# Half of the attention's queries get their scores with keys on partitions

## The chip, the cores and the metric

The kernel runs on one core of a Trainium2 chip. The core has TensorE (PE, the matrix engine, with its weight loads shown apart as PEld), VectorE (DVE), ScalarE (ACT), GpSimd (POOL) and SyncE (SP, which here only issues DMAs); each works through its own instructions in order and waits on semaphores for the others. The metric is the device time of one execution in microseconds (us). Before the change it is 1508.91 us, the median of 3 runs (1508.52 to 1512.15).

## The reference, cut to what matters

The model layer is a linear recurrent unit, a gated feed-forward block, a multi-head attention and the same feed-forward block again, each added to x, which is 4 x 1024 tokens of width 256. The change is in the attention, which has 8 heads of width 64, with keys and values made from one latent of width 64:

```
def _L0_attn_b_ref(x, Wq, Wkv_down, Wk_up, Wv_up, Wo):
    B, T = (4, 512)
    D_MODEL = 256
    N_HEADS = 8
    HEAD_DIM = 64
    ...
    q = (x @ Wq.T).reshape(b, t, N_HEADS, HEAD_DIM)
    kv_latent = x @ Wkv_down.T
    k = (kv_latent @ Wk_up.T).reshape(b, t, N_HEADS, HEAD_DIM)
    v = (kv_latent @ Wv_up.T).reshape(b, t, N_HEADS, HEAD_DIM)
    scale = HEAD_DIM ** (-0.5)
    scores = jnp.einsum('bqhd,bkhd->bhqk', q, k) * scale
    attn = jax.nn.softmax(scores, axis=-1)
    out = jnp.einsum('bhqk,bkhd->bqhd', attn, v)
    out = out.reshape(b, t, N_HEADS * HEAD_DIM)
    return out @ Wo.T
```

Here b is 4 and t is 1024 (the shape of x decides, not the constants). The feed-forward block needs, per token, the 32 largest of 256 softmax scores twice over.

## The kernel before, in words

Everything stays on the chip. There are three stretches: the recurrent unit, the first feed-forward block's first 8 tiles and the attention's weights (to about 356 us); the attention, with the other 24 tiles of the first feed-forward block and the start of the second woven in (to about 1275 us); the second feed-forward block (to the end).

The attention absorbs the key and value matrices into the query and output weights, so that keys and values of all heads are the latent itself. `kh` and `kl` are the rounded latent and its remainder (float32r), with channels on partitions, the 64 channels twice; `qs` holds for each head of a pair the query's rounded part on one half of the partitions and its remainder on the other. So one product with `kh` and one with `kl` sum to almost exact scores.

`heads` (L856) is the main loop. For a batch b, it goes over 2 blocks of 512 queries (nb), 4 pairs of heads (g) and 4 groups of 128 queries (q): 128 units in all, each with two steps, one for each head (j) of the pair; 256 steps in all. A step makes scores `sc` with queries on partitions and 1024 keys in the free dimension (L886, 4 matmuls with 512 columns), their negated maximum `nm` (L890), and the exponentials `pr` with their sum (L894). The value product needs keys on partitions, and here units differ:

- even q (`by_dma`): `pr` is split into two f16 parts `pd` (L897 on ACT, L898 on POOL) and a DMA turns both over (L899, issued by SP) into `d`; the value product takes 48 matmuls in f16;
- odd q: PE turns `pr` over in 8 blocks of 128x128 per step (L905, into `ptp`), ACT copies them out in two halves (L910; in the last batch DVE takes one half, L908), and the value product takes 16 matmuls in f32, which the profile shows as 32.

`values_sum` (L920) does the value product into `pmo` (L930), spreads the reciprocals of the sums over 128 columns (`rows`, L926 on POOL), transposes them on PE (L938), copies them out (L940 on ACT) and multiplies (L941 on DVE) into `on`. It is called some steps after the scores: the lists `pending` and `late` hold back what waits for the copies and for the DMA.

All else in this stretch is side work: `queries` (L842), `output` (L943), `prepare` and `values` for the next batch, feed-forward tiles (`f1.tile`, L589, with its 8 rounds of top-8 in L674, and `nm` on POOL in L613) and `f2.head`. `merge` (L963) sets the order: after each step of `heads` it lets those side generators run whose due step has come, with the due steps written out by hand in L1202 to L1228. The instructions go to the engines through a scheduler that keeps close to this order. PSUM buffers are few: two score buffers `sc` of two banks, two of one bank for turned blocks (`t`), two of one bank for all else (`s`).

## Time and profile before

| what | from | us |
|---|---|---|
| time, median of 3 runs | the times | 1508.91 |
| span of the profiled execution | the page | 1505.6 |
| first stretch, 0 to 356.5 | windows of the trace | 356.5 |
| attention stretch, 356.5 to 1275 | windows of the trace | 918.5 |
| last stretch, 1275 to the end | windows of the trace | 230.6 |

Busy us of each engine in the three stretches, from the same answer:

| stretch | PE | PEld | DVE | ACT | POOL | granted PE clock | DMA share |
|---|---|---|---|---|---|---|---|
| first | 302.23 | 191.71 | 286.50 | 178.25 | 116.94 | 0.95 | 0.17 |
| attention | 822.83 | 655.29 | 689.26 | 704.43 | 429.86 | 0.99 | 0.43 |
| last | 153.37 | 100.30 | 205.19 | 135.31 | 136.17 | 0.82 | 0.06 |

A row of the profile names the line, the engine, the operation, the tile written and those read, the shapes and the count; then the busy time and the mean duration of one; then the idle time of the engine just before such instructions and what ended it. PE's instructions overlap (one starts while the one before it drains), so their mean duration is longer than the distance between them; busy time counts the union.

### The profile page before, as it was taken

Reading aid. Unit: us, or ns where it says so; the run is one execution under the profiler, and the core shown is the slowest. Engines: PE = TensorE matmul, PEld = TensorE weight load, DVE = VectorE, ACT = ScalarE, POOL = GpSimd, SP = SyncE. Lnnn points to the kernel's source line nnn. Section 1 sums busy time; section 2 is a strip of 40 time slices with the busy share of each in tenths; the row PEclk is TensorE's granted clock in tenths of the full one; section 3 lists DMA queues with packets and bytes.
Section 4 is the critical chain, followed back from the end, with each engine's and each line's share of the span. In section 5 each row is a group of like instructions: output and inputs, shape, how many; then the busy total and the mean of one; then the engine's idle time right before and its main releaser. Section 6 shows DMA issues by size and latency. Waiting matters only on the chain. (4 is left out here: it accounts for less than half of the span.)

```text
span 1505.6 us, 28728 instructions
## 1 busy us (share of the span) xinstructions
PE 1278.4 (85%) x10136; PEld 947.3 (63%) x10136; DVE 1181.0 (78%) x3682; ACT 1018.0 (68%) x2152; POOL 683.0 (45%) x849
## 2 busy tenths in 40 slices
PE   4899998887998998898988988889999999576765
PEld 3645555465776777676766766677777877244544
DVE  8988676796778876977777778777676675599998
ACT  5334535666878877787877687877877776566664
POOL 2024523352555454454534543545443534067776
PEclk9999999799999999999999999999999999678898
DMA  3010000432553443353434344433444444000000
GB/s 119 20 55 15 22 21 29 144 105 50 92 88 72 81 86 67 61 89 75 77 73 79 61 69 80 75 74 71 71 85 85 85 85 85 1 15 25 22 25 29
DMA packets 288754, 96.52 MB, mean 64 GB/s; under 512 B 268377, under 2 KB 284770, under 8 KB 288610
## 3 DMA queue, kind: packets, MB, share of 16 engines
q1 hardware_dynamic: 283522, 88.90, 29.6%
q10 hardware_dynamic: 5088, 5.78, 1.1%
q8 instruction: 80, 1.31, 0.4%
q14 instruction: 64, 0.52, 0.1%
HBM read 16.01 MB, written 11.53 MB: 18 GB/s over the span
## 5 line engine op out<-in xcount | busy, mean ns | idle before, releaser
L898 POOL TENSOR_TENSOR pd<-pr,pd 128x1024 f16<-128x1024 f32 x128 | 273.6, 2142 | 259.3 <-ACT pd L897 200.1
L890 DVE TENSOR_REDUCE nm<-sc 128x1 f32<-128x1024 f32 x256 | 308.4, 1217 | 74.8 <-PE sc L886 73.2
L894 ACT ACTIVATE pr<-sc,nm 128x1024 f32<-128x1024 f32 x256 | 286.1, 1120 | 89.8 <-DVE nm L892 54.7
L886 PE MATMUL sc<-kh,qs 128*128 128x512 f32 x512 | 184.4, 438 | 28.5 <-ACT pr L894 21.0
L886 PE MATMUL sc<-kl,qs 128*128 128x512 f32 x512 | 161.7, 396 | 0.0
L674 DVE MATCH_REPLACE8 wk<-m,wk 128x256 f32<-128x256 f32 x384 | 155.3, 408 | 0.1
L910 ACT COPY p<-ptp 128x512 f32<-128x512 f32 x224 | 124.1, 591 | 44.4 <-PE ptp L905 32.5
L674 DVE MAX8 m<-wk 128x8 f32<-128x256 f32 x384 | 150.7, 413 | 0.4
L905 PE MATMUL ptp<-ident,pr 128*128 128x128 f32 x1024 | 139.2, 276 | 13.3 <-ACT pr L894 12.0
L930 PE MATMUL pmo<-p,la 128*64 128x128 f32 x2048 | 140.2, 284 | 5.9 <-ACT ft L524 2.9
L905 PEld LDWEIGHTS ptp<-ident,pr 128*128 128x128 f32 x1024 | 116.2, 141 | 35.5 <-ACT pr L894 21.7
L897 ACT CAST pd<-pr 128x1024 f16<-128x1024 f32 x128 | 133.5, 1054 | 4.6 <-DMA d<-pd 3.6
L930 PEld LDWEIGHTS pmo<-p,la 128*64 128x64 f32 x2048 | 119.6, 142 | 24.7 <-issue 4.7
L886 PEld LDWEIGHTS sc<-kh,qs 128*128 128x128 f32 x512 | 85.2, 195 | 53.9 <-ACT pr L894 32.9
L886 PEld LDWEIGHTS sc<-kl,qs 128*128 128x128 f32 x512 | 96.6, 189 | 23.2 <-issue 1.4
L930 PE MATMUL pmo<-d,lb 128*64 128x128 f16 x3072 | 101.5, 220 | 8.7 <-DVE qs L853 2.6
L930 PEld LDWEIGHTS <-lb 128*64 128x64 f16 x3072 | 90.7, 110 | 26.6 <-issue 19.9
L628 POOL TENSOR_TENSOR ex<-ex,wk 128x512 f32<-128x512 f32 x61 | 77.8, 1276 | 58.4 <-DVE wk L674 48.9
L926 POOL COPY rows<-rs 128x128 f32<-128x128 f32 x128 | 36.3, 297 | 120.4 <-PE pmo L938 71.7
L941 DVE TENSOR_TENSOR on<-pmo,rb 128x128 f32<-128x128 f32 x128 | 36.4, 284 | 64.8 <-ACT rb L940 64.3
L147 PE MATMUL pt<-ident,xn 128*128 128x128 f32 x256 | 48.9, 310 | 44.0 <-ACT xn L145 32.3
L699 PE MATMUL pf<-wf,vt 128*128 128x256 f32 x288 | 80.9, 424 | 3.9 <-ACT vt L697 3.4
(307 smaller groups left out, 2766.1 us busy)
## 6 DMA issues: line engine op xcount, KB each, us to landing
tt<-ft SPq DMA_DIRECT2D x16, 256.0 KB
tt<-tt SPq DMA_DIRECT2D x8, 512.0 KB
out<-x SPq DMA_DIRECT2D x32, 128.0 KB
x<-in_x ACTq DMA_DIRECT2D x6, 512.0 KB
pf<-pfs SPq DMA_DIRECT2D x12, 256.0 KB
full<-pf SPq DMA_DIRECT2D x24, 128.0 KB
d<-pd SPq DMA_TRANSPOSE x128
wa<-in_w_attn SPq DMA_DIRECT2D x2, 640.0 KB
```

Of the source, the lines that this page charges most:

```text
L147: nc.tensor.transpose(pt[:, k, i * P : (i + 1) * P], xn[:, k * P : (k + 1) * P], ident)
L628: pool.tensor_tensor(ex, ex, wk, ALU.subtract)
L674: ins = make(*args).ins
L699: nc.tensor.matmul(dst, vt[:, k, :], w.wf[:, k, :], start=(k == 0 and bias is None), stop=(k == KD - 1))
L886: nc.tensor.matmul(sc[:, sl], qs[:, j, q * P : (q + 1) * P], kk[:, sl], start=(i == 0), stop=(i == 1))
L890: nc.vector.tensor_reduce(nm, sc, AX.X, ALU.max, negate=True)
L894: nc.scalar.activation(pr, sc, AF.Exp, bias=nm, accum_out=ssum[:, j : j + 1])
L897: nc.scalar.copy(pd[:, 0, :], pr)
L898: nc.gpsimd.tensor_tensor(pd[:, 1, :], pr, pd[:, 0, :], ALU.subtract)
L905: nc.tensor.transpose(pt[:, kk, :], pr[:, kc * P : (kc + 1) * P], self.ident)
L910: nc.scalar.copy(dst, pt)
L930: nc.tensor.matmul(po[j * HD : (j + 1) * HD, 0, :], v, pts[j][:, c, :], start=(n == 0), stop=(n == len(terms) - 1),)
```

## The change

Even units stay as they were in what they compute. Odd units (q of 1 and 3) are made differently, in a new class `Turned`:

- `maxima`: a step's scores with queries on partitions, but with `kh` alone (2 matmuls where there were 4), and their negated maximum;
- `begin`: four DMAs on SP's queue build `bq`, 65 partitions of moving data: the rounded queries of both heads on 64 partitions, and on the 65th the negated maxima, which go to DRAM (128 partitions of 2 elements) and come back as one row of 256;
- `chunks`: scores a second time, with keys on partitions and the 2 x 128 queries of both heads in the free dimension: for each block of 128 keys one matmul with `kh` as weights against `qs` and one with `kb` (the 64 channels of `kl` and a row of ones) against `bq`, so that the last contraction row subtracts the maximum. ACT makes the exponentials of two blocks at a time, in f32, directly where the value product needs them; POOL adds the four results into `acc`;
- `values`: the value product from these, 16 matmuls as before, and a copy of the undivided result into `on`.

For both odd units of a group together, `sums` adds `acc` over partitions with a matrix of ones (8 matmuls), takes reciprocals, and spreads them with 8 DMAs into `rb`; `divide` multiplies `on` on POOL. `heads` is replaced by `sweep`, which runs over all 32 groups (a batch, a block and a pair) of 8 steps, with the place of each piece written out: for group n, at step t = 8n, maxima at t, t+2, t+4, t+6, `begin` at t+2.1 and t+6.1, chunks from t+5.1 and t+9.1 on, one per step, values at t+9.5 and t+13.5, sums at t+14.05; the last group has its own places. The due steps of the side work move with it, and `latents` copies `kl` into `kb` by DMA.

The diff, cut; the class `ByDma`, not shown, holds the even units' part of the old loop (with 2 buffers of `pr` for 3), and `values_sum`, now called for even units only, is unchanged.

```diff
+        self.ones = wp.tile([P, 32], F32, tag="ones32", name="ones32")
+        self.nc.gpsimd.memset(self.ones, 1.0)
...
+                wp.tile([HD + 1, T], F32R, tag="kb", name="kb", bufs=2),
             )
+            nc.gpsimd.memset(self.k[b][4][HD : HD + 1, :].bitcast(F32), 1.0)
...
+        nc.sync.dma_start(self.k[b][4][0:HD, to].bitcast(F32), kl[0:HD, to].bitcast(F32))
...
-    def heads(self, b, psum):
...
+    def sweep(self, psum):
+        groups = [(b, nb, g) for b in range(B) for nb in range(2) for g in range(PAIRS)]
+        events = []
+        def at(time, make, *args):
+            events.append((time, len(events), make, args))
+        for n, key in enumerate(groups):
+            t = 8 * n
+            last, before = n == len(groups) - 1, n == len(groups) - 2
+            for i, q in enumerate((0, 2)):
+                unit = self.by_dma(*key, q)
+                for j in range(2):
+                    at(t + (2 * i + j if last else 4 * i + 2 * j + 1), unit.scores, j, psum)
+                at(t + (5 + 2 * i if last else 7 + 4 * i), unit.values, psum)
+            units = [self.turned(*key, q) for q in (1, 3)]
+            for i, unit in enumerate(units):
+                for j in range(2):
+                    at(t - 2.5 + i + 0.5 * j if last else t + 4 * i + 2 * j, unit.maxima, j, psum)
+                at(t + 0.2 + 4 * i if last else t + 2.1 + 4 * i, unit.begin)
+                for c in range(TPB // 2):
+                    at(t + 3 + 2.6 * i + 0.5 * c if last else t + 5.1 + 4 * i + c, unit.chunks, c, psum)
+                at(t + 5 + 2.3 * i if last else t + 9.5 + 4 * i, unit.values, psum)
+            at(t + 8.3 if last else t + 14.05, self.sums, units, psum)
+            at(t + 8.4 if last else t + 14.1 if before else t + 15.95, self.divide, units)
+        events.sort(key=lambda e: e[:2])
+        for step in range(8 * len(groups)):
+            while events[0][0] < step + 1:
+                _, _, make, args = events.pop(0)
+                make(*args)
+            yield
+        for _, _, make, args in events:
+            make(*args)
...
+    def sums(self, units, psum):
+        nc, sp = self.nc, self.sp
+        ps = psum.tile([P, P], "s", "pss")
+        for half in range(2):
+            for i, unit in enumerate(units):
+                for j in range(2):
+                    r = 64 * j + 32 * i
+                    nc.tensor.matmul(
+                        ps[r : r + 32, :], self.ones, unit.acc[:, half, j, :], start=half == 0, stop=half == 1
+                    )
+        rec = sp.tile([P, P], F32, tag="rec", name="rec", bufs=1)
+        nc.vector.reciprocal(rec, ps)
+        rb = self.rb = self.hp.tile([P, 2, P], F32, tag="rb2", name="rb2", bufs=1)
+        for i in range(2):
+            for j in range(2):
+                for half in range(2):
+                    to, of = 64 * j + 32 * half, 64 * j + 32 * i
+                    nc.sync.dma_start(rb[to : to + 32, i, :], rec[of : of + 32, :])
+    def divide(self, units):
+        for i, unit in enumerate(units):
+            self.nc.gpsimd.tensor_tensor(unit.on, unit.on, self.rb[:, i, :], ALU.mult)
...
+class Turned:
...
+    def begin(self):
+        at, nc = self.at, self.at.nc
+        qs = at.qs[self.key]
+        self.bq = at.hp.tile([HD + 1, 2, P], F32R, tag="bq", name="bq", bufs=2)
+        for j in range(2):
+            mine = slice(j * HD, (j + 1) * HD)
+            nc.sync.dma_start(
+                self.bq[0:HD, j, :].bitcast(F32), qs[mine, j, self.q * P : (self.q + 1) * P].bitcast(F32)
+            )
+        rows = at.dram.tile([2, P], F32, tag="nmd", name="nmd", bufs=3)
+        nc.sync.dma_start(rows.rearrange("j p -> p j"), self.nm)
+        nc.sync.dma_start(
+            self.bq[HD : HD + 1].rearrange("o j p -> o (j p)").bitcast(F32),
+            rows.rearrange("(o j) p -> o (j p)", o=1),
+        )
+    def maxima(self, j, psum):
+        at, nc = self.at, self.at.nc
+        kh, qs = at.k[self.key[0]][0], at.qs[self.key]
+        if j == 0:
+            self.nm = at.sp.tile([P, 2], F32, tag="nmt", name="nmt", bufs=4)
+        sc = psum.tile([P, T], "sc", "scm")
+        for kb in range(2):
+            sl = slice(kb * 512, (kb + 1) * 512)
+            nc.tensor.matmul(sc[:, sl], qs[:, j, self.q * P : (self.q + 1) * P], kh[:, sl], start=True, stop=True)
+        nc.vector.tensor_reduce(self.nm[:, j : j + 1], sc, AX.X, ALU.max, negate=True)
+    def chunks(self, i, psum):
+        at, nc, wp = self.at, self.at.nc, self.at.hp
+        kh, kb, qs = at.k[self.key[0]][0], at.k[self.key[0]][4], at.qs[self.key]
+        pt = psum.tile([P, 2, 2, P], "t", "pt")
+        for n in range(2):
+            c = slice((2 * i + n) * P, (2 * i + n + 1) * P)
+            nc.tensor.matmul(pt[:, n], kh[:, c], qs[:, :, self.q * P : (self.q + 1) * P], start=True, stop=False)
+            nc.tensor.matmul(pt[:, n], kb[:, c], self.bq, start=False, stop=True)
+        v = wp.tile([P, 2, 2, P], F32, tag="pe", name="pe", bufs=5)
+        nc.scalar.activation(v, pt, AF.Exp)
+        self.parts = self.parts + [v] if i else [v]
+        if i == 1:
+            self.acc = wp.tile([P, 2, 2, P], F32, tag="acc", name="acc", bufs=2)
+            nc.gpsimd.tensor_tensor(self.acc, self.parts[0], v, ALU.add)
+        elif i > 1:
+            nc.gpsimd.tensor_tensor(self.acc, self.acc, v, ALU.add)
+    def values(self, psum):
+        at, nc = self.at, self.at.nc
+        la = at.k[self.key[0]][2]
+        po = psum.tile([P, P], "s", "pmt")
+        for c in range(TPB):
+            for j in range(2):
+                nc.tensor.matmul(
+                    po[j * HD : (j + 1) * HD, :],
+                    la[:, c, :],
+                    self.parts[c // 2][:, c % 2, j, :],
+                    start=(c == 0),
+                    stop=(c == TPB - 1),
+                )
+        self.on = at.row(self.key, self.q)
+        nc.scalar.copy(self.on, po)
...
-                (n + nb * 32 + 8 * g - 7, at.queries(b, nb, g, psum, "s"), 1)
+                (n + nb * 32 + 8 * g - 3.6, at.queries(b, nb, g, psum, "s"), 1)
...
-            side.append((n + 33, at.output(b, 0, psum), 1.5))
-            if b < B - 1:
-                side.append((n + STEPS + 1.5, at.output(b, 1, psum), 1.5))
-            else:
-                side.append((n + STEPS - 5.5, at.output(b, 1, psum, pairs=slice(0, PAIRS - 1)), 1.5))
-            side.append((n + 40 if b == B - 1 else n + STEPS + 24, f2.head(2 * b, sp, psum, "s"), 2))
+            for nb in range(2):
+                end = n + 32 * nb + 32
+                if b < B - 1 or nb == 0:
+                    side.append((end + 4.3, at.output(b, nb, psum, (0, 2)), 1))
+                    side.append((end + 8.3, at.output(b, nb, psum, (1, 3)), 1))
             last = b == B - 1
+            if last:
+                side.append((n + STEPS - 4.5, at.output(b, 1, psum, (0, 2), slice(0, PAIRS - 1)), 1.5))
+                side.append((n + STEPS - 1.5, at.output(b, 1, psum, (1, 3), slice(0, PAIRS - 1)), 1))
+            side.append((n + 48, f2.head(2 * b, sp, psum, "s"), 2))
             if not last:
-                side.append((n + STEPS + 8, f2.head(2 * b + 1, sp, psum, "s"), 2))
-            if b < B - 1:
+                side.append((n + STEPS + 16, f2.head(2 * b + 1, sp, psum, "s"), 2))
...
-    nc = bacc.Bacc("TRN2", target_bir_lowering=False, num_devices=1)
+    nc = bacc.Bacc("TRN2", target_bir_lowering=False, num_devices=1, dynamic_dma_scratch_size=512)
```

## The prediction

> **What bounds the kernel now.** I read the busy shares on the page first, then the windows of the trace, which say in which stretch the change falls.
>
> ```profile
> PE 1278.4 (85%) x10136; PEld 947.3 (63%) x10136; DVE 1181.0 (78%) x3682; ACT 1018.0 (68%) x2152; POOL 683.0 (45%) x849
> ```
>
> ```profile
> core 0: us, PE busy (x) PEld busy (x) DVE busy (x) ACT busy (x) POOL busy (x), PEclk, DMA share, GB/s
> 715.00:745.00 30.00, 28.43 (x272) 24.00 (x271) 22.71 (x54) 23.34 (x47) 17.20 (x17) 1.00 0.42 81
> 356.50:1275.00 918.50, 822.83 (x8293) 655.29 (x8295) 689.26 (x1719) 704.43 (x1372) 429.86 (x421) 0.99 0.43 78
> ```
>
> In the attention stretch PE is busy for 823 of 918.5 us (90%), at nearly full granted clock; ACT stands at 77%, DVE at 75%, POOL at 47%. PE's work, in its fixed order, is the bound, and only 95.7 us of idle time lie beside it. A good stretch as long as one group of 8 steps, 715 to 745 us, gets down to 5% idle (28.43 of 30). So an edit that only relieves ACT can win part of those 95.7 us and no more; a larger gain needs less work on PE. One step is 918.5 / 256 = 3.59 us, a group of 8 steps 28.7 us. Next, what PE waits for there (us in total, times, longest):
>
> ```profile
> PE sc L886 <- ACT pr L894: 21.0, 23, 2.6
> PE ptp L905 <- ACT pr L894: 12.0, 14, 1.9
> ...
> PE pmo L930 <- DMA d<-pd: 2.5, 5, 0.7
> ```
>
> The first two belong to ACT's queue; the third says that data a DMA turns over, four steps ahead of its use, hardly ever comes late.
>
> **PE's work.** Durations of overlapping matmuls mislead, so I take distances between starts from the timeline of PE (start, length of the row, instruction, count):
>
> ```profile
> 712.61 1.97 PE L930 MATMUL pmo<-p,la 128*64 128x128 f32 x32
> 714.51 0.33 PE L938 MATMUL pmo<-ident,rows 128*128 128x128 f32 x1
> ...
> 719.84 1.59 PE L170 MATMUL pmy<-wvo,onp 128*128 128x256 f32 x12
> 721.27 1.04 PE L905 MATMUL ptp<-ident,pr 128*128 128x128 f32 x8
> ...
> 736.53 0.62 PE L886 MATMUL sc<-kl,qs 128*128 128x512 f32 x2
> 736.99 0.62 PE L886 MATMUL sc<-kh,qs 128*128 128x512 f32 x2
> ...
> 739.61 1.04 PE L905 MATMUL ptp<-ident,pr 128*128 128x128 f32 x8
> 740.40 1.67 PE L170 MATMUL pmy<-wvo,onp 128*128 128x256 f32 x12
> ```
>
> Removed per odd unit (two steps): the `kl` products, 2 x 0.46 (736.99 - 736.53) = 0.92; the transposes, 2 x 0.79 (740.40 - 739.61) = 1.58; the transpose of `rows`, about 0.12 (at most its 0.33). Together 2.62 us, over 64 odd units 168 us. Added: 16 chunk matmuls of 256 columns, each with its own weights. The 12 of `pmy` have that shape and weight pattern and take 1.43 (721.27 - 719.84), 0.119 each, so 1.91. The sums are 8 f32 matmuls, 16 rows, per group; 32 such rows take 1.90 (714.51 - 712.61), so 0.95 per group, 0.48 per unit. Together 2.38 us, 153 us over all. The value products stay 16 per unit. PE saves 168 - 153 = 15 us: the scores made twice eat nearly all that the transposes free. Bounds: the chunks come four at a time, and a pair of score matmuls that opens a run took 0.1 us more than one that follows in it (0.55 from 735.98 to 736.53, against 0.46); 2.5 more openings per unit are 16 us, which leaves nothing saved. At half the distance of the 512-column rows, 0.115, the saving is 19 us. So 0 to 19; I take 15, the row of the same shape.
>
> **The other engines.** Rows of the stretch, by shape:
>
> ```profile
> L890 DVE TENSOR_REDUCE nm<-sc 128x1 f32<-128x1024 f32 x254 | 306.0, 1217 | 72.5 <-PE sc L886 70.8
> L894 ACT ACTIVATE pr<-sc,nm 128x1024 f32<-128x1024 f32 x254 | 283.9, 1120 | 89.8 <-DVE nm L892 54.7 <-DVE nm L890 26.0 <-PE pmo L930 4.5
> L898 POOL TENSOR_TENSOR pd<-pr,pd 128x1024 f16<-128x1024 f32 x128 | 273.6, 2142 | 259.3 <-ACT pd L897 200.1 <-issue 42.3 <-PE pmy L170 4.1
> L910 ACT COPY p<-ptp 128x512 f32<-128x512 f32 x221 | 122.3, 591 | 40.2 <-PE ptp L905 31.9 <-PE pmo L930 7.5
> ...
> L628 POOL TENSOR_TENSOR ex<-ex,wk 128x512 f32<-128x512 f32 x24 | 30.7, 1281 | 25.4 <-DVE wk L674 17.9 <-DVE rs L924 3.7 <-ACT pr L894 3.6
> ```
>
> - ACT, per odd unit: two exponentials (2.24), their accumulator reads (2 x 0.20), 3.5 copies of `p` (2.07) and the copy of `rb` (0.27) go; four exponentials of 128x512 (priced as L910, 2.36) and one 128x128 copy (0.27) come. That is 2.35 less, 150 us in all: 704 becomes 554.
> - DVE: L941 and L924 go (0.284 + 0.153 per unit, 28 us) and the last batch's copies L908 (20 us). Added are 32 reciprocals of 128x128, of which the trace has none: between 0.15 (128x2, L924) and 1.22 (L890, eight times the elements); I take 0.28, the 128x128 L941, so 9 us. About 650 us.
> - POOL: three adds of 128x512 (as L628, 3.84) and a 128x128 product (about 0.4, half of the 0.80 of L658's 128x256), less `rows` (0.30): 3.94 more, 252 us in all. 430 becomes 682, 77% of a stretch of 885 us.
>
> ACT's 150 us were not the bound, so they are worth only PE's waits for ACT: 21.0 + 12.0, and 1.9 for `p`, 35 us. The maxima free their score buffer after DVE's reduction, without an exponential. At the low end the half of the 21.0 that is even units' stays, so 24. ACT's lighter queue could take up to 15 more, from waits for `vt`, `ft`, `ex` and `xn`. I take 35.
>
> **The new waits.** SP's issues:
>
> ```profile
> L899 SPq DMA_TRANSPOSE d<-pd x128: 1468/1914/4143, 365.2 to 1269.6; - x128
> ...
> L599 SPq DMA_DIRECT2D full<-pf x24: 319/325/1277, 344.6 to 982.6; - x24
> ```
>
> A group now issues 4 transpositions and 16 plain DMAs: 4 x 1.91 + 16 x 0.33 = 12.9 of 28.7 us, so the queue isn't full, but it is in order. The chunk that opens a unit waits for `bq`, whose last row goes maximum (1.22), DMA to DRAM, DMA back. By the packets' times in the DMA records, a plain load (`full`) has its last packet 1.9 to 2.9 us after its issue in nine of ten cases, 5.6 in one. With 2.3 each the chain is 1.22 + 4.6 = 5.8 us; the cover is 5.1 - 2 = 3.1 steps, 11.1 us. The 5.3 us over are what it may lose to DVE's queue and to transpositions ahead of it in SP's queue, which themselves wait for POOL's `pd`. If `bq` is late, PE stops in order: the value products, the next scores and with them DVE and ACT follow. The low end is the wait that such a DMA costs today (2.5 us in all), the high end one transposition issue at each odd unit, 64 x 1.91 = 122 us. I take 15, near the low end, since the cover is about twice the chain. The kernel's end gets longer: after the last value product come sums (0.5), reciprocal (0.3), 8 DMA issues (2.6), a landing (2.3) and the product on POOL (0.4), where a transpose, a copy and a product took about 0.9: +5 us. The `kb` copies and memsets lie ahead of their use by many steps; without that cover they would cost some 3 us a batch.
>
> A rule speaks against moving work to POOL. The two rows below overlap:
>
> ```profile
> 803.21 2.05 DVE L64 SCALAR_TENSOR_TENSOR ax_t<-ax_rs 128x4 f32<-128x4 f32 x1
> ...
> 803.10 2.14 POOL L898 TENSOR_TENSOR pd<-pr,pd 128x1024 f16<-128x1024 f32 x1 [3.10 <-ACT pd L897]
> ```
>
> DVE's tiny L64 takes 2.05 us, to the end of POOL's work, where its neighbours take 0.16; L890's 1.22 us are the same with POOL busy or not. The Trainium skill ("SBUF — State Buffer", Terms) says that the port pair which these two engines share is locked for a whole instruction and the loser is blocked. Taken alone, for the 154 DVE instructions of the stretch with two inputs in SBUF, with POOL's busy share up by 0.31 and half of 2.14 us lost each time, it would make 51 us on DVE: 650 becomes 701, 79% of the stretch, still behind PE, so the sum would not move.
>
> **Sum.** -15 (PE) - 35 (waits for ACT) + 15 (`bq`) + 5 (end) = -30, so a span of 1475.6; the median of the runs lies 3.3 over the profiled span (1508.9 against 1505.6), so **1479**. Its own range, from the bounds but with up to 35 us of new waits: 1455 to 1500.
>
> **Rivals.**
> - *`bq` late in SP's queue (slower).* For it: it stands behind transpositions that wait for POOL, the engine that gains 252 us. Against: 5.3 us to spare, and 2.5 us of waits for DMAs now. Without the 15 the sum is -35 - 15 + 5 = -45, so it turns to a loss from 0.7 us per odd unit; one transposition issue at half the units (61) gives 1525, at all (122) 1586. Chance 0.24.
> - *POOL's order becomes a bound (slower).* POOL at 77% also makes `nm` of the feed-forward tiles, for which ACT waits in order (6.7 us now), and `pd`. If at each of the 24 tiles and once in each of the 32 groups one subtraction of 2.14 is in the way, 56 x 2.14 = 120 us fall on ACT or SP and perhaps half on PE: -30 + 60, 1539; with the tiles alone 1530. Against: 23% free. Chance 0.12.
> - *PE fills up (faster).* With ACT at 63%, idle falls to that of 715 to 745: (823 - 15) / 0.948 = 852, -66 + 5: 1448. Against: other waits in that list, for `qs`, stay. Chance 0.12.
> - *Waits only change places:* PE's work the same, new waits as long as those removed: 1509. Chance 0.07.
>
> The forecast itself has 0.45. A change of 0.3% (4.5 us) can be told from none. Faster: 0.45 + 0.12 = 0.57; same 0.07; slower 0.24 + 0.12 = 0.36. The range 1445 to 1545 leaves out the upper half of the first rival (0.12) and some of the third.
>
> **What will show it.** In the new profile: chunk matmuls at 0.12 us between starts, PE busy near 808 us in the stretch; ACT near 554, POOL near 682; waits of PE for `pr` gone for odd units; waits of the chunk line for DMA `bq` near 15 us. Wrong would be: 60 us or more of PE waiting for `bq` or `d`; chunks above 0.15 apart (32 us more); ACT waiting long for POOL's `nm`.

## The result, and the profile after

The changed kernel takes 1886.92 us, the median of 4 runs (1882.59 to 1888.43), beside 1510.10 us for the kernel before in the same comparison (1508.52 to 1512.15): a ratio of 1.2481, with a 95% interval of 1.2455 to 1.2507. The profiled execution has a span of 1886.4 us. The forecast was 1479, within 1445 to 1545.

First the page of the changed kernel: the busy shares, the row of PE in the 40 slices, and two groups of instructions (busy us, mean ns of one, then the idle time in front of them and what ended it).

```profile
PE 1357.9 (72%) x10328; PEld 1015.2 (54%) x10328; DVE 1201.5 (64%) x3554; ACT 908.9 (48%) x1928; POOL 936.0 (50%) x1046
...
PE   5899969766577767677776777765876668656666
...
L1056 PE MATMUL pt<-bq,kb 65*128 65x256 f32 x512 | 159.1, 334 | 254.6 <-DMA bq<-nmd 206.7
...
L1058 ACT ACTIVATE pe<-pt 128x512 f32<-128x512 f32 x256 | 147.9, 598 | 305.4 <-PE pt L1056 276.8
```

No engine is the bound any more: PE fell from 85% to 72%, and POOL, which the change loads, has 50%. PE stood for 254.6 us in front of one line, the chunk matmul that reads `bq`, and ACT in turn for 276.8 us behind that line. Where the time lies is seen in the window from the first score product to the last value product, the attention without what surrounds it, before and after:

```profile
core 0: us, PE busy (x) PEld busy (x) DVE busy (x) ACT busy (x) POOL busy (x), PEclk, DMA share, GB/s
356.60:1281.20 924.60, 828.98 (x8396) 660.50 (x8397) 691.22 (x1723) 706.06 (x1377) 430.15 (x422) 0.99 0.43 77
```

```profile
359.70:1655.70 1296.00, 907.95 (x8562) 727.54 (x8562) 709.45 (x1593) 596.52 (x1151) 679.93 (x614) 0.82 0.44 62
```

The attention took 371 of the 381 us of span. PE's idle time in it rose from 95.6 us to 388 (1296.00 - 907.95), and its busy time by 79, at a granted clock of 0.82 for 0.99. SP's queue shows where the row is held up. Its timeline over one group, from one `rb` to the next (start, length of the row, DMA issued, count):

```profile
816.76 5.51 SPq L930 DMA_DIRECT2D rb<-rec  x8
822.40 1.68 SPq L1008 DMA_TRANSPOSE d<-pd  x1
824.18 1.17 SPq L1030 DMA_DIRECT2D nmd<-nmt  x1
834.47 0.25 SPq L1031 DMA_DIRECT2D bq<-nmd  x1
834.84 2.80 SPq L1008 DMA_TRANSPOSE d<-pd  x1
837.74 1.17 SPq L1026 DMA_DIRECT2D bq<-qs  x2
839.00 1.53 SPq L1030 DMA_DIRECT2D nmd<-nmt  x1
848.72 0.25 SPq L1031 DMA_DIRECT2D bq<-nmd  x1
849.06 3.07 SPq L1008 DMA_TRANSPOSE d<-pd  x1
852.23 1.17 SPq L1026 DMA_DIRECT2D bq<-qs  x2
853.49 2.91 SPq L1008 DMA_TRANSPOSE d<-pd  x1
856.50 4.99 SPq L930 DMA_DIRECT2D rb<-rec  x8
```

L1030 writes the maxima to DRAM, L1031 reads them back as a row and has to wait until the write is complete. Between the two issues lie 10.29 us (834.47 - 824.18) and 9.72 us, in which SP issues nothing else. 20.01 us of the group's 39.74 (856.50 - 816.76) go so, and the other rows fill 18.81 more (5.51 + 1.68 + 0.25 + 2.80 + 1.17 + 0.25 + 3.07 + 1.17 + 2.91): 38.8 of 39.7 us, so in this group SP's queue is full. It is the fullest of all. Over the whole attention SP issues for 593 us and stands for 412 in front of the 64 read-backs (from the end of the issue before to the start of the read-back's), 1005 of 1296 us or 78%; whether this sets the time is asked with e17. Over all 64 pairs the distance between the two issues is 8.1 us at least, 9.7 in the middle and 20.2 at most; in 41 of them SP gets other DMAs issued in between. On PE the first of these two looks like this (in brackets the idle time in front of an instruction and what ended it):

```profile
828.74 0.28 PE L1055 MATMUL pt<-qs,kh 128*128 128x256 f32 x1
837.76 0.58 PE L1056 MATMUL pt<-bq,kb 65*128 65x256 f32 x1 [8.73 <-DMA bq<-nmd]
```

The row issued at 834.47 released PE at 837.76, 3.3 us later. PE had stood 8.73 us.

### The profile page after: what moved, and what is told of

It reads as the page before. It is cut to its first block, busy times and chain, and to the rows that moved or that the text cites. A ratio compares the mean times of both kernels' runs of the same rounds, so it can differ in the third digit from the quotient of the medians.

```text
span 1886.4 us, 29996 instructions
## 1 busy us (share of the span) xinstructions
PE 1357.9 (72%) x10328; PEld 1015.2 (54%) x10328; DVE 1201.5 (64%) x3554; ACT 908.9 (48%) x1928; POOL 936.0 (50%) x1046
## 4 chain that ended last, share of the span: by engine, by line
DVE 29%; DMA 26%; PE 22%; issue 9%; ACT 7%; POOL 4%; SPq 3%; another core or an unknown queue 0%; DVEq 0%; ACTq 0%; POOLq 0%
DMA nmd<-nmt 12%; DMA d<-pd 8%; DVE wk L674 6%; DVE m L674 5%; DMA bq<-nmd 3%; PE pmt L1073 3%; PE sc L999 2%; DVE nmt L1046 2%; PE pt L1056 2%; SPq L930 2%; DVE nm L1001 2%; PE pmo L947 2%; PE pmq L170 1%; DMA rb<-rec 1%; PE pt L1055 1%
## 5 line engine op out<-in xcount | busy, mean ns | idle before, releaser
L1056 PE MATMUL pt<-bq,kb 65*128 65x256 f32 x512 | 159.1, 334 | 254.6 <-DMA bq<-nmd 206.7
L1058 ACT ACTIVATE pe<-pt 128x512 f32<-128x512 f32 x256 | 147.9, 598 | 305.4 <-PE pt L1056 276.8
L1001 DVE TENSOR_REDUCE nm<-sc 128x1 f32<-128x1024 f32 x128 | 156.2, 1220 | 210.4 <-PE sc L999 209.9
L1056 PEld LDWEIGHTS pt<-bq,kb 65*128 65x128 f32 x512 | 115.3, 229 | 268.5 <-issue 135.9
L1004 ACT ACTIVATE pr<-sc,nm 128x1024 f32<-128x1024 f32 x128 | 142.7, 1115 | 118.2 <-DVE nm L1002 100.9
L1046 DVE TENSOR_REDUCE nmt<-scm 128x1 f32<-128x1024 f32 x128 | 155.5, 1216 | 36.0 <-PE scm L1045 35.5
L1055 PE MATMUL pt<-qs,kh 128*128 128x256 f32 x512 | 158.9, 330 | 17.6 <-ACT pe L1058 17.5
L1064 POOL TENSOR_TENSOR acc<-acc,pe 128x512 f32<-128x512 f32 x128 | 163.6, 1279 | 10.3 <-ACT pe L1058 6.0
L1073 PE MATMUL pmt<-pe,la 128*64 128x128 f32 x2048 | 143.8, 298 | 27.5 <-DVE xnt L161 17.7
L1073 PEld LDWEIGHTS pmt<-pe,la 128*64 128x64 f32 x2048 | 125.5, 150 | 48.5 <-DVE xnt L161 18.1
L1062 POOL TENSOR_TENSOR acc<-pe 128x512 f32<-128x512 f32 x64 | 81.9, 1279 | 116.7 <-ACT pe L1058 70.7
```

Source lines behind the costliest of these rows:

```text
L1001: nc.vector.tensor_reduce(nm, sc, AX.X, ALU.max, negate=True)
L1004: nc.scalar.activation(pr, sc, AF.Exp, bias=nm, accum_out=self.ssum[:, j : j + 1])
L1046: nc.vector.tensor_reduce(self.nm[:, j : j + 1], sc, AX.X, ALU.max, negate=True)
L1055: nc.tensor.matmul(pt[:, n], kh[:, c], qs[:, :, self.q * P : (self.q + 1) * P], start=True, stop=False)
L1056: nc.tensor.matmul(pt[:, n], kb[:, c], self.bq, start=False, stop=True)
L1058: nc.scalar.activation(v, pt, AF.Exp)
```

## The experiments

Each ratio is against the kernel before, run on the same chip beside it. The last three columns are taken from the first score product to the last value product of the profiled execution.

| kernel | us, median | ratio (95%) | attention, us | PE busy in it | granted clock |
|---|---|---|---|---|---|
| before | 1510 to 1513 | 1 | 924.6 | 829.0 | 0.99 |
| changed | 1886.92 | 1.2481 (1.2455 to 1.2507) | 1296.0 | 908.0 | 0.82 |
| e1 row through PE | 1563.75 | 1.0333 (1.0311 to 1.0356) | 969.2 | 838.2 | 0.94 |
| e2 constant row | 1551.39 | 1.0255 (1.0217 to 1.0293) | 954.2 | 821.7 | 0.93 |
| e5 whole pieces | 1651.82 | 1.0917 (1.0870 to 1.0964) | 1057.2 | 859.8 | 0.90 |
| e17 later read | 1729.49 | 1.1440 (1.1388 to 1.1492) | 1132.9 | 883.9 | 0.86 |
| e18 = e5 + later read | 1615.16 | 1.0684 (1.0634 to 1.0734) | 1019.9 | 856.5 | 0.91 |
| e6 no adds | 1554.20 | 1.0267 (1.0229 to 1.0305) | 958.0 | 833.4 | 0.94 |
| e7 order alone | 1506.96 | 0.9956 (0.9937 to 0.9975) | 921.8 | 833.8 | 0.97 |
| e9 ones columns | 1616.43 | 1.0681 (1.0643 to 1.0718) | 1025.9 | 905.8 | 0.95 |
| e10 no last sums | 1550.35 | 1.0250 (1.0221 to 1.0280) | 962.1 | 835.3 | 0.94 |
| e11 norm early | 1539.11 | 1.0164 (1.0129 to 1.0199) | 942.1 | 829.3 | 0.95 |
| e12 = e10 + e11 | 1523.03 | 1.0070 (1.0049 to 1.0091) | 941.5 | 831.8 | 0.95 |
| e13 = e7 + e11 | 1490.51 | 0.9860 (0.9828 to 0.9893) | 907.0 | 826.2 | 0.98 |
| e14 tiles early | 1576.88 | 1.0415 (1.0378 to 1.0452) | 983.5 | 847.7 | 0.94 |
| e15 = e7 + e14 | 1517.22 | 1.0031 (1.0015 to 1.0046) | 932.2 | 843.4 | 0.96 |
| e16 bare | 1523.97 | 1.0063 (1.0037 to 1.0090) | 932.5 | 818.5 | 0.94 |

### The trip through DRAM

**e1: the row without DMAs.** The maxima are spread to 66 columns on ACT, transposed on PE so that they land on partition 64, and copied into `bq` by ACT.

```diff
-        nc.sync.dma_start(rows.rearrange("j p -> p j"), self.nm)
-        nc.sync.dma_start(
-            self.bq[HD : HD + 1].rearrange("o j p -> o (j p)").bitcast(F32),
-            rows.rearrange("(o j) p -> o (j p)", o=1),
-        )
...
+    def shift(self, psum):
...
+        nc.scalar.copy(wide[:, 0 : HD + 1], self.nm[:, 0:1].to_broadcast([P, HD + 1]))
+        nc.scalar.copy(wide[:, HD + 1 : HD + 2], self.nm[:, 1:2])
+        for j in range(2):
+            nc.tensor.transpose(ps[0 : HD + 1, j, :], wide[:, j : j + HD + 1], at.ident)
+        nc.scalar.copy(self.bq[HD : HD + 1], ps[HD : HD + 1])
```

> The row of shifts is made on PE instead of by two DMAs through DRAM: ACT spreads each maximum over 65 columns, two PE transposes put it on partition 64, ACT copies 1x256 into bq; the two DMAs go, all else stays. Theory A (the trip through DRAM, some 9.7 us from issuing its write to issuing its read back, 64 times, stops SP and then PE): most of the 377 us go, 1480 to 1540 us, and PE's waits for bq fall from 335 us (PE and its weight loads) to under 40. Theory B (POOL's 250 us of adds and the longer chain of engines are the cause, and the wait for bq is only where it shows): another wait takes its place, over 1700 us.

1563.75 us: 323 of the 377 us go, and PE no longer waits for `bq` by a DMA. The trip through DRAM is the cause of that part. The new way has a price of its own: ACT's busy time in the attention is 640 us, where it was 597. And the time stays 3.3% above the kernel before, 24 us over the range that theory A gave, so the trip isn't all of the loss.

**e2: no shift at all.** This one leaves the computing of the shift out, with a constant in its place.

```diff
+        nc.vector.memset(self.bq[HD : HD + 1].rearrange("o j p -> o (j p)").bitcast(F32), -1.0)
...
-        nc.scalar.activation(v, pt, AF.Exp)
+        nc.scalar.activation(v, pt, AF.Exp, scale=0.01)
```

> Leaves out the shift: the 65th row is set to a constant by DVE, the exponential is scaled by 0.01 to stay finite, and no maximum leaves the chip; the maxima are still computed. Theory A: within 20 us of the run with the row made on PE, rather below it, since two copies, two transposes and a PSUM buffer go too. Theory B: over 1700 us. If this one falls and the run with PE does not, the latency of any way from the maximum to the row is the cause, not the DMAs.

1551.39 us, 12 less than e1, although DVE now fills the row, 64 times 0.27 us. Without any wait for a shift the change is still 2.6% slower than the kernel before.

**e4: such trips on an idle queue.** The kernel before, with pairs of DMAs at its very end, each issued when the one ahead of it is complete: 4 times the scattered write of the changed kernel (`tda`) and the read-back, 4 times a write of 8 bytes per partition in one piece (`tdb`), then larger copies.

```diff
+    da = dram.tile([2, P], F32, tag="tda", name="tda")
+    db = dram.tile([P, 2], F32, tag="tdb", name="tdb")
...
+        (da.rearrange("j p -> p j"), s2, row, da.rearrange("(o j) p -> o (j p)", o=1)),
+        (db, s2, row, db.rearrange("(o p) j -> o (p j)", o=1)),
...
+            for dst, src in ((to, of), (back, again)):
+                with tc.issue_after(last) if last else nullcontext():
+                    last = nc.sync.dma_start(dst, src).ins
```

> The kernel before, with four kinds of dependent DMA pairs at its very end, four times each, on an otherwise idle queue: 128x2 elements of 4 bytes written to DRAM with the partition innermost and read back as a row (as in the change), the same with 8 bytes per partition in one piece, 64x128 from SBUF to SBUF and back, 128x128 to DRAM and back. Theory A1 (the scattered write itself is slow): 7 us or more from its issue to the issue of the read back, about 2.5 us for the others. Theory A2 (it is slow only because it stands behind transpositions on the DMA engines): 2 to 3 us here for all kinds, as the plain loads showed before the change.

The timeline of SP at the end of that kernel:

```profile
1511.79 0.38 SPq L985 DMA_DIRECT2D tda<-ts  x1
1519.83 0.25 SPq L985 DMA_DIRECT2D trow<-tda  x1
1523.26 0.39 SPq L985 DMA_DIRECT2D tda<-ts  x1
...
1554.98 0.33 SPq L985 DMA_DIRECT2D tdb<-ts  x1
1558.33 0.23 SPq L985 DMA_DIRECT2D trow<-tdb  x1
1560.44 0.33 SPq L985 DMA_DIRECT2D tdb<-ts  x1
...
1598.10 0.32 SPq L985 DMA_DIRECT2D twide<-tdd  x1
1599.91 0.32 SPq L985 DMA_DIRECT2D tdd<-twide  x1
1601.44 0.32 SPq L985 DMA_DIRECT2D twide<-tdd  x1
```

With nothing beside it, the scattered write of 1 KB needs 8.04 us (1519.83 - 1511.79; 8.0 to 8.1 in all four) until what waits for it can be issued, and reading the row 3.4 to 3.7 more. The same kilobyte in pieces of 8 bytes needs 2.8 to 4.1 us, a write of 64 KB in whole rows 1.53 (1601.44 - 1599.91). So the write is slow by its form, 256 pieces of 4 bytes, and not by what stands in SP's queue; in its place in the changed kernel it takes 1.7 us more (9.7 - 8.0). Whether the size of a piece counts, their number or their places in DRAM wasn't told apart. By the packets' times in the DMA records, its packets end 1.1 to 1.2 us after the issue in all four cases, so the last packet isn't what the read-back waits for. The Trainium skill ("DMA: Bandwidth & Descriptors", Anatomy of one DMA — SWDGE (gpsimd) path) gives DMAs of GpSimd's path a fixed cost of about 2.0 us, most of it the confirmation that the last byte has landed. These DMAs are SP's; a completion long after the packets agrees with the records, but 2.0 us would be far from the 8.0 measured.

**e5: the same trip in whole pieces.** DRAM holds the maxima as [128, 2], the read-back gathers.

```diff
-        rows = at.dram.tile([2, P], F32, tag="nmd", name="nmd", bufs=3)
-        nc.sync.dma_start(rows.rearrange("j p -> p j"), self.nm)
+        rows = at.dram.tile([P, 2], F32, tag="nmd", name="nmd", bufs=3)
+        nc.sync.dma_start(rows, self.nm)
...
-            rows.rearrange("(o j) p -> o (j p)", o=1),
+            rows.rearrange("p (o j) -> o j p", o=1),
```

> The changed kernel with one thing altered: the two DMAs of the shift stay on SP's queue, but the one that writes to DRAM puts 8 bytes of each of the 128 partitions in one piece ([128, 2] in DRAM) where the changed kernel scatters 256 pieces of 4 bytes ([2, 128]); the one that reads back gathers the row of 256 from it. In the run on the idle queue the scattered write took 8.1 us and the one in whole pieces 2.8 to 4.1 us. Theory A1 (the scattered write is what is late): the trip falls from some 13 us to about 7, under the cover of 11.1 us, PE's waits for bq fall from 335 us (matmul and weight load) to under 40 us, and the time comes to that of the kernel whose shift goes through PE (1564 us), 1535 to 1590 us. Rival A3 (any trip of the shift through DRAM stalls PE here, because SP stands still between its two DMAs with the transpositions behind it): over 1650 us, and the waits for bq or d stay over 150 us.

1651.82 us: a change of one layout wins 235 us, so the form of the write is most of it, as A1 says. Yet the time is as high as A3 had it, and the waits lie between the two. The waits of SP (for the write) and of PE (for the row), us in total, times and the longest:

```profile
SPq L1031 <- DMA nmd<-nmt: 103.6, 50, 4.3
```

```profile
PE pt L1056 <- DMA bq<-nmd: 86.3, 27, 7.1
```

In the changed kernel these were 387.9 and 206.7. The two issues now lie 4.0 us apart in the middle of all pairs (3.6 where SP issues nothing in between), but PE still waits 86 us. The trace shows where the row's time goes. From the end of a unit's second maximum to the issue of its write pass 3.7 us in the middle, and up to 14.8, because SP is still at other DMAs; then 4.0 to the read-back, and 3.8 until the row releases PE (3.3 to 4.4, but for one case of 6.1; in the changed kernel 3.3). With the maximum of 1.22 that is 12.7 us, about the cover of 3.1 steps (11.1 us at the step of before, 12.8 at this kernel's), so a longer delay in SP's queue can reach PE.

**e17 and e18: is SP's queue the bound, or the latency of the trip?** By its latency the trip costs 9.7 + 3.5 = 13.2 us, or 14.4 with the maximum, against a cover of 11.1 us: 64 x 2.1 = 134 us, or 64 x 3.3 = 211, not 323. e17 keeps the scattered write and puts the read-back behind one transposition more in SP's order, so that SP issues other DMAs meanwhile while the row lands later. e18 does this to e5, half a step earlier (t + 4.1).

```diff
-        nc.sync.dma_start_transpose(self.pts[j], pd.rearrange("p i k -> p (i k)"))
+        at.turn = nc.sync.dma_start_transpose(self.pts[j], pd.rearrange("p i k -> p (i k)")).ins
...
+                at(t + 0.3 + 4 * i if last else t + 4.6 + 4 * i, unit.back)
...
+    def back(self):
+        nc, rows = self.at.nc, self.rows
+        with self.at.tc.issue_after(self.at.turn):
+            nc.sync.dma_start(
+                self.bq[HD : HD + 1].rearrange("o j p -> o (j p)").bitcast(F32),
+                rows.rearrange("(o j) p -> o (j p)", o=1),
+            )
```

> The changed kernel with its scattered write, the read-back queued on SP behind one more of the even units' transpositions than in the changed kernel, so that SP issues other DMAs while the write completes. A trip of 9.7 + 3.5 = 13.2 us is 2.1 us longer than the cover of 11.1 us, which would make 64 x 2.1 = 134 us, but 323 us went with it. Theory J (SP's queue is full: it stands 9.7 us at each of 64 trips, 620 us, and issues 128 transpositions at 1.9 us, 245 us, and some 500 plain DMAs at 0.33 us, 165 us, 1030 us in all against 925 us of the stretch): with SP free during the write the time falls clearly, to 1620 to 1780 us, though each read-back lands later. Theory K (only the latency of the trip counts): the read-back lands later than before and the time rises over 1890 us.

> The kernel that writes the shift in whole pieces of 8 bytes (1652 us), with the same later place of the read-back. There SP stands only some 3.3 us a trip, 210 us, and the queue's sum is some 620 us of 925. Theory J: SP isn't the bound here, so the later place wins nothing and its later landing costs: 1650 to 1730 us, and near the run before it in this call. Theory K: slower by the delay of the read-back, some 3 to 4 us at each of 64 trips: over 1800 us.

e17 takes 1729.49 us, 157 less than the changed kernel, in the range of theory J; latency alone would have made it slower. For the row does come later: the read-back is issued 13.8 us after the write in the middle, where it was 9.7, and the chunk that needs it starts 22.9 us after the maximum, where it was 19.9. But SP's standing in front of the read-backs falls from 412 to 89 us. (The sum in the expectation, 1030 us, took 9.7 us of standing at each trip; that is too much, since SP often has other DMAs to issue.) The waits of SP and PE in it:

```profile
SPq L1037 <- DMA nmd<-nmt: 75.9, 16, 7.4
```

```profile
PE pt L1062 <- DMA bq<-nmd: 130.8, 28, 7.9
```

So the changed kernel loses its time twice over at the same DMA: 157 of the 323 us come from SP's standing, which delays all that is queued behind it, and they go although the row lands later. The other 166 belong to the late row and to what SP still stands; these two weren't told apart. e18 missed what theory J expected: 1615.16 us, 37 less than e5, where no gain was expected. There SP's standing fell from 109 to 13 us. So standing costs time though the queue isn't full on the average.

### The other 51 us

**e6, e7, e9: POOL's adds or the order?** All start from e1, except e7, which has the changed kernel's order for all but the odd units' own pieces (transposes from t+2.1 and values at t+5.8, where the changed kernel has chunks from t+5.1 and values at t+9.5) and the work of the kernel before.

e6:

```diff
-        if i == 1:
-            self.acc = wp.tile([P, 2, 2, P], F32, tag="acc", name="acc", bufs=2)
-            nc.gpsimd.tensor_tensor(self.acc, self.parts[0], v, ALU.add)
-        elif i > 1:
-            nc.gpsimd.tensor_tensor(self.acc, self.acc, v, ALU.add)
...
-                        ps[r : r + 32, :], self.ones, unit.acc[:, half, j, :], start=half == 0, stop=half == 1
+                        ps[r : r + 32, :], self.ones, self.fixed, start=half == 0, stop=half == 1
```

e7, in `Turned`:

```diff
-            nc.tensor.matmul(pt[:, n], kh[:, c], qs[:, :, self.q * P : (self.q + 1) * P], start=True, stop=False)
-            nc.tensor.matmul(pt[:, n], kb[:, c], self.bq, start=False, stop=True)
...
-        nc.scalar.activation(v, pt, AF.Exp)
...
+            nc.tensor.transpose(pt[:, kk, :], self.prs[j][:, kc * P : (kc + 1) * P], at.ident)
+        nc.scalar.copy(self.pts[j][:, 4 * half : 4 * half + 4, :], pt)
```

e9, where the second half of `la` holds ones:

```diff
-                wp.tile([P, TPB, HD], F32, tag="la", name="la", bufs=2),
+                wp.tile([P, TPB, 2 * HD], F32, tag="la", name="la", bufs=2),
...
+                po, la[:, c, :], self.parts[c // 2][:, c % 2], start=(c == 0), stop=(c == TPB - 1)
...
+        nc.vector.reciprocal(rec, po[HD:, :, :])
+        on = at.row(self.key, self.q)
+        for j in range(2):
+            nc.vector.tensor_tensor(on[j * HD : (j + 1) * HD], po[0:HD, j, :], rec[:, j, :], ALU.mult)
```

> The kernel with the shift through PE (1564 us), without POOL's adds of the exponentials: the sums are made over a tile that is filled once, so this leaves out the softmax sums of the odd groups; the matmuls, the reciprocal, the DMAs and the product of the sums stay. Theory B (the 250 us of adds on POOL cost the time that is left over before, by holding the ports that the small instructions of DVE wait for, and by making POOL late): POOL's busy time in the stage falls from 680 to some 430 us, DVE's by 15 to 30 us, and the time to 1515 to 1540 us. Rival C (the new order of the work, with half-units interleaved and side work at other steps, costs it): 1550 to 1568 us.

> The order of the changed kernel with the work of the kernel before: the sweep by events, its steps for scores and values, and its due steps for the side work stay, but the odd groups are made as before (both score products, exponential with its sum, transposes on PE, copies by ACT); no second scores, no DMA of a shift, no adds on POOL. Rival C (the order costs what is left): 1530 to 1560 us against 1510 us. Theory B (POOL's adds and the other new work cost it): 1500 to 1520 us.

> The kernel with the shift through PE (1564 us), with the sums made by the value product itself: the values get 64 columns of ones, so that one matmul of 128x128 by 256 columns gives values and sums for both heads; POOL's adds, the matmuls of the sums, the four DMAs that spread the reciprocal and POOL's product are gone, DVE takes a reciprocal of 64x256 and two products of 64x128 for each unit. PE loses 0.28 us a unit (half of the 0.57 us of the sums' matmuls), some 18 us; POOL 280 us; DVE gains some 0.9 us a unit, 58 us, less 30 us for the reciprocal that goes and less what the ports give back. Theory B: 1505 to 1535 us. Rival C: 1540 to 1560 us, that is no more than PE's own saving.

e6: 10 us less than e1, under what theory B expected, though POOL's busy time fell to 442 us and DVE's by 13 (699.9 to 686.8). The adds are a small part. e7: 1506.96 us, 0.44% faster than the kernel before (0.25 to 0.63%), so the new order costs nothing, and rival C falls, but for the later places of the odd units' pieces, which e7 doesn't have. It is the fastest kernel here that computes all of the layer.

e9 was meant to beat both and missed. The rows of its value product and of its reciprocal, and below them the value product of e1:

```profile
L1045 PE MATMUL pmt<-pe,la 128*128 128x256 f32 x896 | 209.3, 388 | 3.5 <-ACT xc_f L533 3.2 <-DVE qs L858 0.3
...
L1049 DVE RECIPROCAL rec<-pmt 64x256 f32<-64x256 f32 x57 | 100.2, 1758 | 45.5 <-PE pmt L1045 44.5
```

```profile
L1079 PE MATMUL pmt<-pe,la 128*64 128x128 f32 x1940 | 122.4, 278 | 6.7 <-ACT xc_f L533 5.5 <-DVE on L959 0.9 <-DVE qs L859 0.3
```

The expectation took a product with 128 output rows to cost what two with 64 cost. Per unit it is 16 instructions in 3.7 us (209.3 / 56) against 32 in 2.0 (122.4 / 60.6): by this half the pairs with 64 rows, for the two heads, run side by side. The Trainium skill ("TensorEngine Tiling (Array Packing)", When to Use Tiling) says of weights with 64 columns or fewer that two such tiles share the array; the two rows agree with it. The reciprocal of 64x256 takes 1.76 us.

**e10 to e12: the end, and the late norm.** e10 leaves the sums and the division of the last two groups out; e11 makes the layer norm of the next batch three steps earlier.

```diff
-            at(t + 8.3 if last else t + 14.05, self.sums, units, psum)
-            at(t + 8.4 if last else t + 14.1 if before else t + 15.95, self.divide, units)
+            if not (last or before):
+                at(t + 14.05, self.sums, units, psum)
+                at(t + 15.95, self.divide, units)
```

```diff
-                side.append((n + 38, chain(at.prepare(b + 1, 0, psum, "s"), at.values(b + 1, 0, psum, "s")), 1.5))
-                side.append((n + 56, chain(at.prepare(b + 1, 1, psum, "s"), at.values(b + 1, 1, psum, "s")), 1.5))
+                side.append((n + 35, chain(at.prepare(b + 1, 0, psum, "s"), at.values(b + 1, 0, psum, "s")), [4.5] + [1.5] * 6))
+                side.append((n + 53, chain(at.prepare(b + 1, 1, psum, "s"), at.values(b + 1, 1, psum, "s")), [4.5] + [1.5] * 6))
```

> The kernel with the shift through PE (1564 us), without the sums and the division of the odd groups in the last two groups of heads: this leaves out their softmax division. In its last two groups the attention takes 76.5 us where the kernel before takes 55.3 us, and PE stands some 4.6 us and 5 us there between the matmuls of the sums and the output product. Theory D (the new chain after the sums, that is reciprocal, DMAs, POOL's product and the cast for the output, stands behind the end of the attention with nothing left to cover it): the last two groups fall by 10 to 18 us and the time to 1545 to 1555 us. Rival E (the end is slow by the order of its chunks and value products, not by the sums): under 5 us, 1558 to 1565 us.

> The kernel with the shift through PE (1564 us), with the layer norm of the next batch made three steps earlier and its transposes left at their steps. PE stands there for 9.3, 9.3 and 7.1 us in front of the transposes of xn, since DVE reaches the norm late; in the kernel before the longest such wait is 2.1 us. Theory F (the norm on DVE is late by its place among DVE's work): the three waits fall under 3 us each and the time by 12 to 20 us, to 1544 to 1552 us. Rival G (DVE's work in these stretches sets the time, wherever the wait shows): the wait moves to another instruction and the time stays within 5 us of 1564 us.

> Both of the two edits before together (no sums and no division of the odd groups in the last two groups, norm three steps earlier). If both theories D and F hold, the savings add: 1526 to 1542 us. If only one holds, the time is that of the better one alone, 1544 to 1555 us; if neither, 1558 to 1566 us.

e10 takes 13 us off e1, as theory D said, and it does so at its place: from the first score product of the last two groups to the last output product it takes 81.9 us, e1 96.3. The same stretch takes 81.5 and 82.4 us in e12 and e16, which have this edit, and 95.0 to 98.0 in e2, e6, e11 and e14, which don't. The timeline of PE at the end of e1 shows the sums' matmuls and the next output products, which wait for reciprocal, DMAs, POOL's product and ACT's cast:

```profile
1318.01 0.64 PE L921 MATMUL pss<-acc,ones 128*32 128x128 f32 x16
...
1326.01 0.79 PE L170 MATMUL pmy<-wvo,onp 128*128 128x256 f32 x2 [4.59 <-ACT onp L970]
...
1334.16 0.64 PE L921 MATMUL pss<-acc,ones 128*32 128x128 f32 x16
...
1340.67 1.01 PE L170 MATMUL pmy<-wvo,onp 128*128 128x256 f32 x3 [5.23 <-ACT onp L970]
```

e11 seemed to show theory F, with 25 us less, and so did e12 with 41. But in both, and in e13, the early norm reads the last four tiles before the feed-forward addition of the last of them is in, so that a dependency is gone with the place; their times are not those of a usable kernel. Their expectations didn't reckon with it.

**e13 to e15: place or dependency?** e13 is the edit of e11 on e7. e14 and e15 move the feed-forward tiles by three steps along with the norm, on e1 and on e7, which keeps the dependency.

```diff
-            start = 1 + 6.75 * n if n < TPB else STEPS * (n // TPB) - STEPS + 48.25 + 8 * (n % TPB + 1)
+            start = 1 + 6.3 * n if n < TPB else STEPS * (n // TPB) - STEPS + 45.25 + 8 * (n % TPB + 1)
```

> The kernel with the new order and the old work (1507 us), with the norm three steps earlier as well. It has two waits of 3.9 and 3.0 us in front of the transposes of xn. Theory F: 2 to 8 us less, 1499 to 1505 us. Rival G: 1505 to 1510 us.

> The kernel with the shift through PE (1564 us), with the first mixer's tiles and the norm behind them both three steps earlier. In the run before, the norm alone was moved, so that it read the last four tiles ahead of the last one's addition: that run took a dependency away as well. Here it is kept. Theory F (the norm is late by the place of its tile and itself among DVE's work): most of the 25 us of that run are kept, 1538 to 1550 us, and the waits for xn stay under 3 us each. Rival H (that run was faster only because the norm no longer waited for the last tile): the waits come back and the time is 1555 to 1568 us.

> The kernel with the new order and the old work (1507 us), with the same move of the first mixer's tiles and the norm by three steps, its dependency kept. Theory F: 1488 to 1500 us, faster than the kernel before by 0.8 to 1.5%. Rival H: 1503 to 1510 us.

e13 gained 16 us with the old work too, so most of e11's gain has nothing to do with the change. e14 took 1577 us and e15 1517, 13 and 10 more than the kernels they start from. In e14 the long waits for `xn` are gone from PE's list, against rival H; yet the time didn't fall. Waits of PE from 560 us on to the end of the attention, e1 first, then e14:

```profile
PE pt L147 <- ACT xn L145: 31.7, 10, 9.3
PE pmy L170 <- ACT onp L970: 12.8, 6, 5.2
```

```profile
PE pmy L170 <- ACT onp L970: 12.0, 9, 4.6
PE pmo L948 <- DVE rec L925: 11.8, 8, 3.2
```

The wait only changed its place, as e11's rival G had it: PE's idle time is 135.8 us, where it was 131.0 in e1. What rose is its busy time, by 9.5 us for the same number of instructions (9.6 in e15 over e7); why, is open. These two runs also show what a rearrangement alone is worth here: 10 to 13 us. Single edits of that size can't be told from it by their time alone, which holds for e2 and e6.

**e16: the bare change.** No shift, no adds, no sums for the last two groups (e2, e6 and e10 together).

> The kernel with a constant row (1551 us), without POOL's adds and without the sums and the division of the last two groups: this leaves out the shift, the softmax sums of the odd groups (they are made over a fixed tile) and the division of the last two groups. What is left of the change is the second scores, the chunks with their contraction row and their exponentials. If the three parts add (row through PE 12 us, adds 10 us, sums at the end 13 us off 1564 us): 1524 to 1533 us, still 12 to 20 us over the kernel before, and the bare change has no gain of its own. If it has the gain that the prediction gave to PE (15 us off and no waits for ACT): below 1510 us.

1523.97 us. The parts add up about: 12.4 + 9.6 + 13.4 = 35.4 expected off e1, 39.8 measured. The window of the attention:

```profile
359.20:1291.70 932.50, 818.54 (x8554) 651.14 (x8554) 700.43 (x1656) 588.75 (x1152) 441.64 (x420) 0.94 0.47 86
```

PE works 10.4 us less than in the kernel before (818.54 for 828.98), at a clock of 0.94 for 0.99, and stands 18.3 us more (113.96 for 95.62). Among its waits are new ones, first in e16, then the first of them in the kernel before:

```profile
PE pt L147 <- ACT xn L145: 19.6, 9, 8.1
PE sc L1002 <- DVE nmt L1044: 11.9, 13, 2.0
...
PE sc L1002 <- ACT pr L1007: 6.2, 11, 1.0
```

```profile
PE pt L147 <- ACT xn L145: 1.5, 3, 0.6
```

So the change without its shift, its adds and its last sums gains nothing here. It isn't free of all that serves it: the sums of the other 30 groups stay (on DVE 30 reciprocals, 28.6 us; on POOL 60 products, 27.7 us; 240 DMAs on SP), and the constant row gives DVE 64 fills of 0.27 us that the changed kernel doesn't have. What second scores and chunks would bring alone isn't shown.

## Why the prediction was wrong

The step that failed is the one on the new waits, where the prediction took `bq` at +15 us. It priced the landing of each of the two DMAs at 2.3 us, after the plain load `full`, and so had a chain of 5.8 us under a cover of 11.1. The write alone took 8.0 us on an idle queue and 9.7 in place, the read 3.3 to 3.7: with the maximum of 1.22 some 14 to 15 us. From the maximum to the issue of the write another 5.8 us pass in the middle (17.8 at most), more than the 5.3 that the prediction had to spare. The landing was read from the last packet, and that isn't the completion: in e4 the write's packets end by 1.2 us and the read-back can go at 8.0. And a load of 1 KB to each partition said nothing of 256 pieces of 4 bytes that go the other way; the trace of before held no DMA of that kind. The high end, one transposition issue a unit, was priced after SP's queue and not after the DMA itself, so the range couldn't hold it. Its sign of being wrong came: 206.7 us of PE's waiting for `bq`, where 60 were the mark.

The same step counted SP's queue as 12.9 us a group, issues alone. They took 18.5 (593 / 32): a plain issue was priced at 0.33 us, after `full`, and those of `rb` and of the queries take 0.59 and 0.55 in the middle. And a read-back that waits for a write holds the queue, in order, until the write is complete: 12.9 us more a group (412 / 32). This was left out though the prediction said that the queue is in order. By e17, 157 of the 323 us are due to it.

The sum also held PE's clock as it was. PE was forecast near 808 us and was busy for 908, at 0.82 for 0.99: of the 371 us by which the attention grew, 79 are PE's work at the lower clock and 292 its idle time.

The first rival, `bq` late in SP's queue, had the place and the chain of effects (value products, next scores, DVE and ACT follow), but its price, 1525 to 1586, rested on the same rows. Its cause, the DMAs ahead in the queue, holds for the 5.8 us before the write; the larger part, by e4, is the trip itself.

The other terms, point by point:

- PE, -15 us: 10.4 less in e16, within 0 to 19, at a lower clock; the chunk matmuls start 0.12 us apart, as taken. Right in size.
- Waits for ACT, -35 us: the named ones went (in e16 `sc` waits 6.2 us for `pr`, where it was 21.0, and no `ptp` is left), but others took their place (`sc` now waits 11.9 us for the maxima of DVE) and PE's idle time rose by 18. This is the rival that waits only change places, at 0.07, for the bare change. As a size of a gain the 35 us failed; that idle time falls with the length of a wait list wasn't supported by anything.
- End, +5 us: 14 us in e10 (96.3 - 81.9). The reciprocal of 128x128 took 0.95 us (taken at 0.28), the 8 DMA issues 5.0 to 5.5 in the rows above (taken at 2.6), and the sums of the last but one group are caught by the same chain.
- Busy times: POOL 680 (682 forecast), ACT 597 (554), DVE 709 (about 650). ACT was 42 us over: its instructions' durations, added up, fell by 154 us, as forecast (825.3 to 670.8), but they overlap, and the prediction took them off a busy time that counts the union. On DVE 32 x 0.67 = 21 us of the excess are the reciprocal's. None of them became the bound, and the rival of POOL's order fell: without the adds 10 us go. (Its 1530 for the tiles alone took all of 24 x 2.14 = 51 us, where the 1539 beside it took half; by half it is 1505.)
- The rule of the Trainium skill ("SBUF — State Buffer", Terms) that a lock on shared ports blocks the loser for a whole instruction was estimated at 51 us. By the groups of the trace, the 232 small instructions of DVE with operands in SBUF (norms and the scaling of top values) took 77 to 93 us in the attention of the seven kernels without the adds (78 before) and 91 to 109 in the ten with them, 84 and 101 in the mean: that agrees with the rule, at some 17 us.

What stays open: why the new waits of e16 arise, since each new arrangement of the same instructions moves the time by 10 us or more; and how the 166 us that e17 leaves divide between the late row and SP's queue.

## What to carry to other kernels

Price a DMA by its completion, the issue of what waits for it, and not by its last packet, and by the row nearest in its form (bytes in one piece, direction, the number of pieces), not by its bytes; where the trace has none, the high end must come from the operation itself. A DMA that waits for another one on the same queue holds up all that is queued behind it, so its wait belongs to the queue's sum as much as an issue does. And a relief of an engine that is not the bound is worth what a run shows and not the length of the waits named after it, which the next wait in the list can take over whole.

## What the runs showed of the hardware

- A write to DRAM of 128 x 2 f32, scattered in pieces of 4 bytes, lets what waits for it be issued 8.0 to 8.1 us after its issue on an idle queue, though its packets end by 1.2 (e4); in pieces of 8 bytes 2.8 to 4.1; 64 KB in rows of 512 bytes 1.5.
- The granted clock of PE in the attention went down as the share of its idle time went up, though not strictly: 0.96 to 0.99 in four kernels with 9 to 10% idle time, 0.93 to 0.95 with 12 to 14%, 0.91 with 16%, 0.90 with 19%, 0.86 with 22%, 0.82 with 30%. Over the same 8562 matmuls PE was busy 822 us at 0.93 (e2), 860 at 0.90 (e5) and 908 at 0.82 (changed).
- 32 f32 instructions of 128 columns with 64 output rows each (e1) took 2.0 us a unit, 16 of 256 columns with 128 output rows (e9) 3.7.
- An issue on SP took 0.33 us in the middle for `full` before (128 x 256 f32) and 0.59 for `rb` in the changed kernel (32 x 128 f32).
- A reciprocal from PSUM takes 0.95 us for 128x128 and 1.76 us for 64x256, where a product of 128x128 takes 0.28.
